# A list scheduler that takes the results of GpSimd's masks as ready later: four graph layers on one core

## The chip, the cores and the metric

The kernel runs on one core of a Trainium2 chip. A core has five engines, each with its own instruction stream: TensorE (PE in the profile, with its weight loads shown apart as PEld), VectorE (DVE), ScalarE (ACT), GpSimd (POOL) and SyncE (SP), which here only issues DMA transfers. The engines run beside each other and wait for each other through semaphores. The metric is the time of one execution on the device in microseconds; the figure for a kernel is the median of its runs.

## The reference

There are 128 small graphs. Each has 128 nodes, 512 features a node in `x`, and a 128 by 128 matrix of edges `adj` of zeros and ones. Four attention layers follow each other, and each ends in a residual sum and a layer norm:

```python
x = _layernorm(x + _L0_gnn_ref(x, adj, ...), axis=-1)   # one head; scores from x itself; mask adj + eye
x = _layernorm(x + _L1_gnn_ref(adj, x, ...), axis=-1)   # 4 heads of 256, elu, then one head of 512; softmax over axis 1
x = _layernorm(x + _L2_gnn_ref(x, adj, ...), axis=-1)   # 8 heads of 64
x = _layernorm(x + _L3_gnn_ref(x, adj, ...), axis=-1)   # one head, elu
```

A layer's attention is, with small differences from layer to layer:

```python
e = leaky_relu(s_src[..., :, None] + s_dst[..., None, :], 0.2)
attn = softmax(where(mask, e, -big))
out = einsum(attn, h)        # h is x or x @ W
```

The mask of the first layer is `adj` with the diagonal added. The second layer normalises over the other axis and so needs the transposed mask, diagonal included. The third and fourth layers take `adj` as it is. All is done in float32.

## The kernel before, in words

One graph is one tile of 128 partitions (its nodes). `graph(g)` (L562) writes down the operations of graph g as a list of objects `Op`: an engine, a cost in microseconds, the buffers read and written, and a function that emits the instructions. There are 188 operations a graph, taken by number in the text where a line is not enough. A program of two stages then lays down one order for all engines.

`Pipeline.plan` (L79) places the operations of one model graph in a period of 28 us (`PERIOD`), so that every engine's operations fit in it without overlap; a graph starts every period, and some 18 graphs are in flight together. It uses the costs and the latencies of the table `LATENCY`. Its results are planned times, one for each operation.

`Pipeline.order` (L145) then walks through all operations of all graphs. It keeps a clock for each engine, and at each step issues the operation that can start first by its own estimate of costs. An operation is ready when the operations it depends on have ended plus a delay from the table `FLOW`: one for readers on the same engine, one for readers on another. It looks at most 30 us ahead of the oldest planned operation not yet issued (`AHEAD`). It also chooses the place of each buffer: a place is free once all users of the buffer before it have ended plus the same delay. Eight places are the banks of PSUM, the others lie in SBUF or, for transposition, in DRAM. The order so found is emitted as it stands: on the chip every engine runs its own instructions in that order, and waits where something is not ready. The estimates have no other effect on the program than the order and the places of buffers.

The parts that matter here:

- `first(g)` (L830) is the first layer. It loads x and adj by SyncE (L834, L835). GpSimd adds the diagonal (L838) and makes two masks with `mask` (L737, instruction L738): m0 from the sum and m2 from adj. TensorE transposes m2 through a product with the identity (L850), VectorE multiplies the result by one minus the identity into m1 (L851). m0 serves the first layer, m1 the two attentions of the second, m2 the eight heads of the third; the fourth layer loads adj again and makes its own mask m3.
- `attend` (L632) is the attention: ScalarE's leaky relu (L641), VectorE's masking with the running minimum (L649, one instruction and one accumulator read a head), ScalarE's exponential with its sum (L658), VectorE's reciprocal (L666), in the second and fourth layers GpSimd's scaling (L668), then the transposition in `turned` (L597): VectorE by blocks of 32 (L602), out to DRAM and back by SyncE (L607, L612, L617).
- `norm` (L673): VectorE's statistics (L676, L677), GpSimd's inverse root (L680, L681), then the scaling on VectorE (L699) or, with a further operation of GpSimd (L688, L692), on ScalarE (L695).
- `project` (L704) multiplies by the weights of the second layer (L710 on w1s) and of the third (L710 on wha, eight products a graph, evicted by VectorE at L715 and ScalarE at L717).
- `halves` (L749) does the second weight matrix of the second layer for two graphs at a time with sums made on GpSimd (L780) and products (L794); `mixed` (L722, instruction L725), L896 and L938 are the products with the attention. GpSimd also adds biases and residuals (L862, L881, L950, L986).
- A product in float32 is two matmul instructions, L850 is one.

In `mask` the operation has a cost of 0.8 and no extra; only SyncE's transfers have one, which `Op.done` (L70) adds to the latency in the plan. In `order` it enters only, through `done`, into how many places the buffers of a kind get.

Of the kernel before, what the change touches and what calls it, by code (L numbers as in the profile page):

```python
# [29 lines left out]

PERIOD = 28.0
LATENCY = {"PE": (0.0, 0.8), "DVE": (0.15, 1.6), "ACT": (0.1, 1.6), "POOL": (0.1, 1.6), "SP": (6.8, 6.8)}
FLOW = {"PE": (0.0, 0.6), "DVE": (0.15, 0.9), "ACT": (0.1, 0.9), "POOL": (0.1, 0.9), "SP": (3.2, 3.2)}
AHEAD = 30.0
URGENCY = 0.3
BANKS = 8
# [24 lines left out]
class Op:  # L61
# [7 lines left out]

    def done(self, reader=None):  # L70
        own, other = LATENCY[self.engine]
        return self.cost + self.extra + (own if reader is self.engine else other)


class Pipeline:
# [69 lines left out]
    def order(self, events):  # L145
# [33 lines left out]
        free = {tag: [(0.0, s) for s in range(BANKS if tag == "ps" else len(p))] for tag, p in free.items()}  # L179
        ready, released, clock, lane = [0.0] * n, {}, {e: 0.0 for e in FLOW}, 0.0  # L180
        known = {e: [i for i in range(n) if not before[i] and ops[i].engine == e] for e in FLOW}
        issued, low, out = [False] * n, 0, []

        def start(i):
            t = max(clock[ops[i].engine], ready[i])
            for b in makes[i]:

                rank = 0
                for q in coming[b.tag]:
                    if q >= i or rank >= len(free[b.tag]):  # L190
                        break
                    rank += 1
                if rank >= len(free[b.tag]):
                    return None
                t = max(t, free[b.tag][rank][0])
            return t

        while len(out) < n:
            best = None
            for e, waiting in known.items():  # L200
                found = None
                for i in waiting:
                    if events[i][0] > events[low][0] + AHEAD and i != low:
                        break
                    t = start(i)
                    if t is not None and (found is None or t < found[0]):
                        found = (t, i)
                        if t <= clock[e]:
                            break
                if found and (best is None or found < best):  # L210
                    best = found
            t, i = best
            op = ops[i]
            known[op.engine].remove(i)
            issued[i] = True
            out.append((events[i][1], op))
            for b in makes[i]:
                b.slot = free[b.tag].pop(0)[1]
                coming[b.tag].remove(i)
            clock[op.engine] = done = t + op.cost  # L220
            own, other = FLOW[op.engine]
            if op.dma:

                done = lane = max(lane, done) + op.dma
                own = other = FLOW["SP"][0]
            for q in after[i]:
                ready[q] = max(ready[q], done + (own if ops[q].engine == op.engine else other))
                before[q] -= 1
                if not before[q]:
                    insort(known[ops[q].engine], q)  # L230
            for b in op.bufs:
                released[b] = max(released.get(b, 0.0), done + other)
                open_uses[b] -= 1
                if not open_uses[b] and b.slot is not None and b.tag != "const":
                    insort(free[b.tag], (released[b], b.slot))
            while low < n and issued[low]:
                low += 1
# [4 lines left out]
def tile_gat_stack(  # L242
# [319 lines left out]
    def graph(g):  # L562
# [3 lines left out]
        def op(engine, cost, emit, ins=(), outs=(), extra=0.0, uses=(), dma=0.0):  # L566
            ops.append(Op(engine, cost, emit, list(ins), list(outs), extra, uses, dma))
# [55 lines left out]
        class Col:  # L623
# [3 lines left out]
            def __call__(self, h=None):  # L627
                if h is None:
                    return self.buf.ap[:, self.a : self.a + self.n]
                return self.buf.ap[:, self.a + h : self.a + h + 1]  # L630

        def attend(db, h0, nh, src, mask, scaled=False):  # L632


# [102 lines left out]
        def mask(m, a, what):  # L737
            op("POOL", 0.8, lambda: nc.gpsimd.tensor_scalar(  # L738
                out=m.ap, in0=a.ap, scalar1=0.0, scalar2=-BIG, op0=what, op1=ALU.mult
            ), [a], [m])  # L740

        def score(xv, wv, init, sc, s):
            jk = Buf("junk", [P, F])
# [86 lines left out]
        def first(g):  # L830
# [7 lines left out]
            op("POOL", 0.6, lambda: nc.gpsimd.tensor_tensor(out=ae.ap, in0=at.ap, in1=eye_i, op=ALU.add), [at], [ae])  # L838

            mask(m0, ae, ALU.is_equal)  # L840


# [3 lines left out]
            score(x0, w0s, b0t, sc0, 0)  # L846
            db = spread(Col(sc0, 1, 1), 1)
            mask(m2, at, ALU.is_le)
            pm = bank()
            op("PE", 0.11, lambda: nc.tensor.transpose(pm.ap[:, :P], m2.ap, ident), [m2], [pm])  # L850
# [138 lines left out]
        if g == B:  # L989

            whole = graph(None)
            a = [op.wait for op in whole].index(-1)
# [12 lines left out]
        a = len(ops)  # L1005
# [45 lines left out]
```

## Time and profile before

| | us |
|---|---|
| median of 3 runs | 3205.73 (3203.74 to 3207.6) |
| profiled execution, its own time | 3213.19 |
| its span in the profile | 3211.2 |
| TensorE busy | 3050.0 (95%) |
| VectorE busy | 2967.3 (92%) |
| ScalarE busy | 2172.0 (68%) |
| GpSimd busy | 2285.5 (71%) |
| DMA, mean busy share in the steady stretch | 0.80 |
| granted clock of TensorE, mean | 0.98 |

The profile is one execution. A group is written as line, engine, operation, and the names of what it writes and reads. A wait is written as "who, line <- released by whom, line: us in total, times, longest". Up to about 200 us the weights are loaded and prepared, and after about 3050 us the last graphs run out; between lies the steady stretch, in which one graph leaves every 23.8 us on average (2850 us over some 120 graphs). In the profile an operation that waits shows the idle time in front of it in square brackets.

### The profile page before, as it was taken

The numbers are of one execution on the slowest core, as the hardware profiler recorded it, in microseconds if no ns is written. First come the engines' busy times: TensorE is split into PE (matmuls) and PEld (weight loads), VectorE is DVE, ScalarE is ACT, GpSimd is POOL, SyncE is SP. The second block draws the span as 40 slices with busy tenths as digits, with TensorE's granted clock in tenths as the row PEclk, the third lists the DMA queues.
The fourth block names the chain that finished last, engine by engine and source line by source line (L and its number), as shares of the span: only waits on it lengthen the run. The fifth ranks groups of instructions, "written<-read, shape, count | busy, mean of one in ns | idle before, by whom it ended". The sixth has DMA issues, their size and how long they took to land. (4 is left out here: it accounts for less than half of the span.)

```text
span 3211.2 us, 62683 instructions
## 1 busy us (share of the span) xinstructions
PE 3050.0 (95%) x14822; PEld 2483.6 (77%) x14822; DVE 2967.3 (92%) x10185; ACT 2172.0 (68%) x7427; POOL 2285.5 (71%) x3211
## 2 busy tenths in 40 slices
PE   7899999999999999999999999999999999999974
PEld 4688877788878878788788787887888878878852
DVE  6978999999999999999999999999999999999985
ACT  1356667677777777777777767777777777777764
POOL 3566777777777777777777777777777777777654
PEclk8999999999999999999999999999999999999985
DMA  4457787787888887888788888887787777878784
GB/s 117 104 147 189 190 196 192 192 202 193 204 192 197 202 194 198 197 197 200 193 198 201 192 203 199 194 204 193 198 200 195 200 197 195 203 190 205 183 192 110
DMA packets 1657572, 606.13 MB, mean 189 GB/s; under 512 B 1311562, under 2 KB 1508170, under 8 KB 1657204
## 3 DMA queue, kind: packets, MB, share of 16 engines
q1 hardware_dynamic: 1655836, 598.97, 75.9%
q8 instruction: 120, 1.97, 0.3%
q14 instruction: 248, 2.03, 0.2%
q0 software_dynamic: 576, 2.10, 0.2%
q10 hardware_dynamic: 792, 1.06, 0.1%
HBM read 374.43 MB, written 227.48 MB: 187 GB/s over the span
## 5 line engine op out<-in xcount | busy, mean ns | idle before, releaser
L658 ACT ACTIVATE w<-w,nm 128x128 f32<-128x128 f32 x1920 | 754.2, 394 | 389.5 <-DVE nm L649 347.3
L710 PE MATMUL ps<-w1s,w 128*128 128x258 f32 x4096 | 940.3, 383 | 7.1 <-DMA w<-scr 7.1
L710 PEld LDWEIGHTS ps<-w1s,w 128*128 128x128 f32 x4096 | 780.7, 191 | 176.8 <-issue 30.0
L794 PE MATMUL ps<-w2s,w 128*128 128x257 f32 x3584 | 872.5, 382 | 8.3 <-POOL w L780 5.8
L649 DVE CUSTOM_DVE_ANT_0 w<-w,w 128x128 f32<-128x128 f32 x1920 | 853.6, 545 | 14.4 <-ACT w L641 12.1
L794 PEld LDWEIGHTS ps<-w2s,w 128*128 128x128 f32 x3584 | 655.7, 190 | 98.1 <-POOL w L780 8.0
L602 DVE STREAM_TRANSPOSE w<-w 128x512 f32<-128x512 f32 (+1 forms) x1024 | 539.2, 540 | 45.9 <-POOL w L668 43.8
L710 PE MATMUL ps<-wha,w 128*128 128x273 f32 x2048 | 518.4, 397 | 4.7 <-DMA w<-scr 4.2
L695 ACT ACTIVATE w<-w,mr,rd 128x512 f32<-128x512 f32 x384 | 311.5, 812 | 298.8 <-POOL mr L688 207.2
L641 ACT ACTIVATE w<-w,xl 128x128 f32<-128x128 f32 x1536 | 480.4, 389 | 35.0 <-DMA w<-row 32.4
L710 PEld LDWEIGHTS ps<-wha,w 128*128 128x128 f32 x2048 | 389.2, 195 | 134.9 <-issue 35.6
L950 POOL TENSOR_TENSOR w<-z,w 128x512 f32<-128x512 f32 x128 | 151.7, 1185 | 348.1 <-DVE z L942 301.1
L680 POOL TENSOR_SCALAR rd<-mv 128x1 f32<-128x1 f32 x512 | 153.3, 299 | 341.2 <-DVE mv L677 184.5
L681 POOL TENSOR_TENSOR rd<-rd,neghalf 128x1 f32<-128x1 f32 x512 | 345.7, 675 | 42.7
L658 ACT ACTIVATION_READ_ACCUMULATOR w<-w,nm 128x1 f32 x1920 | 361.4, 188 | 0.0
L676 DVE BATCH_NORM_STATS2 st<-w 128x6 f32<-128x512 f32 x512 | 340.7, 675 | 10.3 <-POOL w L986 6.3
L717 ACT COPY xl<-ps 128x258 f32<-128x258 f32 (+1 forms) x640 | 226.4, 363 | 153.5 <-PE ps L710 152.7
L881 POOL TENSOR_TENSOR xl<-xl,b1t 128x512 f32<-128x512 f32 x256 | 325.1, 1290 | 0.3
L725 PE MATMUL ps<-w,w 128*128 128x512 f32 x512 | 271.7, 613 | 37.4 <-DMA w<-scr 26.5
L938 PEld LDWEIGHTS ps<-xl,w 128*128 128x128 f32 x2048 | 263.1, 195 | 37.4 <-DVE nm L649 12.8
L649 DVE DVE_READ_ACCUMULATOR2_ANT nm<- 128x1 f32 x1920 | 288.2, 150 | 0.0
L938 PE MATMUL ps<-xl,w 128*128 128x66 f32 x2048 | 256.0, 274 | 18.0 <-DMA w<-scr 11.9
(183 smaller groups left out, 4452.1 us busy)
## 6 DMA issues: line engine op xcount, KB each, us to landing
scr<-w SPq DMA_DIRECT2D x640, 256.0 KB
w<-scr SPq DMA_DIRECT2D x640, 256.0 KB
w<-row SPq DMA_DIRECT2D x128, 512.0 KB
w<-in_x_dram SPq DMA_DIRECT2D x128, 256.0 KB
w<-row SPq DMA_DIRECT2D x128, 256.0 KB
out_dram<-w SPq DMA_DIRECT2D x128, 256.0 KB
w<-row SPq DMA_DIRECT2D x384, 64.0 KB
scr<-w SPq DMA_DIRECT2D x384, 64.0 KB
```

Of the source, the lines that this page charges most:

```text
L602: op("DVE", 0.12 + 0.133 * n, lambda: nc.vector.transpose(zb.ap.rearrange("p b h c -> p h b c"), src.ap.rearrange("p (h b c) -> p h b c", ...
L641: nc.scalar.activation(z.ap[:, h, :], db.ap[:, h0 + h, :], AF.Prelu, bias=src(h0 + h), alpha=SLOPE)
L649: nc.vector.tensor_tensor_reduce(out=zz.ap[:, h, :].rearrange("p (b a) -> p a b", b=4), in0=z.ap[:, h, :].rearrange("p (a b) -> p a b", b= ...
L658: nc.scalar.activation(zz.ap[:, h, :], zz.ap[:, h, :], AF.Exp, bias=nm.ap[:, h : h + 1], scale=-1.0, accum_out=rs.ap[:, h : h + 1],)
L676: op("DVE", 0.6, lambda: nc.vector.bn_stats(st.ap, y.ap), [y], [st])
L681: nc.gpsimd.tensor_tensor(out=rd.ap, in0=rd.ap, in1=neghalf, op=ALU.pow)
L695: op("ACT", 0.6, lambda: nc.scalar.activation(y.ap, y.ap, AF.Identity, bias=mr.ap, scale=rd.ap), [y, rd, mr], [y])
L710: op("PE", w * 4 / 2400 + 0.006, lambda k=k: nc.tensor.matmul(px.ap[:, :w], lhsT=lhs.ap[:, k, :], rhs=wa(k, c), start=(k == 0), stop=(k == ...
L725: op("PE", width * 4 / 2400, lambda: nc.tensor.matmul(pa.ap[:, :width] if len(xv.shape) == 2 else pa.ap.rearrange("p (s c) -> p s c", s=2) ...
L794: return lambda: nc.tensor.matmul(q[b].ap[:, :C2], lhsT=x()[:, k, :], rhs=w2s[:, slot, k, :], start=(fresh and k == 0), stop=(k == 3), ski ...
L881: op("POOL", 1.3, lambda nh=nh: nc.gpsimd.tensor_add(xl.ap[:, nh, : 2 * FH], xl.ap[:, nh, : 2 * FH], b1t[:, nh * 2 * FH : (nh + 1) * 2 * F ...
L938: op("PE", 0.225, lambda u=u, h=h: nc.tensor.matmul(pa.ap[:, u * CH : (u + 1) * CH], lhsT=pt.ap[:, u, :], rhs=xl3.ap[:, h * CH : (h + 1) * ...
```

## The change

The change is in the scheduler's estimates, not in what is computed. GpSimd's delay to readers on other engines in `FLOW` goes from 0.9 to 1.2 us. The masks get an extra of 2.0 us, and `order` adds the extra of a GpSimd operation to the delay for readers on other engines, and so also to the time at which the places of the buffers that the mask uses come free. `Op.done` leaves out the extra of all but SyncE's operations, so that the plan is what it was. Two lines are added in `order`, so that what stands behind them (L222 on) has a number higher by two in the changed kernel: the mask is L740 there, the transposition L852.

```diff
-FLOW = {"PE": (0.0, 0.6), "DVE": (0.15, 0.9), "ACT": (0.1, 0.9), "POOL": (0.1, 0.9), "SP": (3.2, 3.2)}
+FLOW = {"PE": (0.0, 0.6), "DVE": (0.15, 0.9), "ACT": (0.1, 0.9), "POOL": (0.1, 1.2), "SP": (3.2, 3.2)}
...
     def done(self, reader=None):
         own, other = LATENCY[self.engine]
-        return self.cost + self.extra + (own if reader is self.engine else other)
+        return self.cost + (self.extra if self.engine == "SP" else 0.0) + (own if reader is self.engine else other)
...
             clock[op.engine] = done = t + op.cost
             own, other = FLOW[op.engine]
+            if op.engine == "POOL":
+                other += op.extra
...
         def mask(m, a, what):
             op("POOL", 0.8, lambda: nc.gpsimd.tensor_scalar(
                 out=m.ap, in0=a.ap, scalar1=0.0, scalar2=-BIG, op0=what, op1=ALU.mult
-            ), [a], [m])
+            ), [a], [m], 2.0)
```

## The prediction

> **What bounds the kernel now.** I read the busy times first, then the waits of TensorE and VectorE over the steady stretch, then the timeline of one graph. From the head of the page:
>
> ```profile
> PE 3050.0 (95%) x14822; PEld 2483.6 (77%) x14822; DVE 2967.3 (92%) x10185; ACT 2172.0 (68%) x7427; POOL 2285.5 (71%) x3211
> ```
>
> From the table by stages, 200 to 3050 us (length, then busy time of PE, PEld, DVE, ACT, POOL; clock; DMA share):
>
> ```profile
> 200.00:3050.00 2850.00, 2788.19 (x13818) 2295.53 (x13817) 2694.33 (x9289) 2022.73 (x6944) 2112.57 (x2957) 1.00 0.80 196
> ```
>
> TensorE is busy 97.8% of the stretch at full clock, VectorE 94.5%. TensorE is idle 61.8 us, VectorE 155.7. The waits of TensorE in that stretch, all of them:
>
> ```profile
> PE ps L850 <- POOL w L738: 58.4, 101, 2.2
> PE ps L794 <- POOL w L780: 2.4, 3, 1.3
> PE ps L710 <- ACT w L641: 0.3, 1, 0.3
> PE ps L710 <- DMA w<-scr: 0.3, 1, 0.3
> ```
>
> So 58.4 of 61.8 us is one wait, 0.58 us at 101 transpositions of a mask (L850) for GpSimd's mask (L738). That wait is the ceiling of the gain. The waits of VectorE in the same stretch, longest first:
>
> ```profile
> DVE w L602 <- POOL w L668: 40.5, 105, 1.8
> DVE w L699 <- POOL rd L681: 28.3, 57, 0.8
> DVE w L851 <- PE ps L850: 17.0, 38, 0.8
> ...
> DVE xl L715 <- PE ps L710: 7.2, 35, 1.8
> ```
>
> A wait on a busy engine may still be a symptom, so I followed one graph in the timeline (start, length, engine, line):
>
> ```profile
> 1498.87 0.18 DVE L677 BATCH_NORM_AGGREGATE mv<-st 128x2 f32<-128x6 f32 x1
> ...
> 1499.21 0.22 POOL L680 TENSOR_SCALAR rd<-mv 128x1 f32<-128x1 f32 x1 [1.38 <-DVE mv L677]
> ...
> 1506.89 0.66 POOL L738 TENSOR_SCALAR w<-adj 128x128 f32<-128x128 int32 x1
> ...
> 1507.61 0.33 PE L850 MATMUL ps<-ident,w 128*128 128x128 f32 x1 [0.58 <-POOL w L738]
> ...
> 1507.63 1.40 POOL L668 TENSOR_TENSOR w<-w,ri 128x512 f32<-128x512 f32 x2
> ...
> 1507.97 0.29 DVE L851 TENSOR_TENSOR w<-ps,noneye 128x128 f32<-128x128 f32 x1
> ...
> 1508.71 0.90 DVE L602 STREAM_TRANSPOSE w<-w 128x512 f32<-128x512 f32 x2 [0.35 <-POOL w L668]
> ```
>
> VectorE's mean and variance (L677) releases GpSimd at 1499.21. GpSimd then works without a gap through ten operations to the first L668, 1508.71 less 1499.21: 9.50 us. There VectorE, which waited 0.35, starts again (L602) and works without a gap to the next L677 of the same kind, which ends at 1523.27; GpSimd starts at 1523.43. 9.50 + 14.56 + 0.16 = 24.22 us, one graph. This is a closed loop of VectorE and GpSimd without TensorE. TensorE's mask hangs on the same run of GpSimd: L738 ends at 1507.55, L850 starts 0.06 later, and the matmuls behind it end in time for VectorE's L715. The two ways round are nearly equal, and both are tight. Emptying TensorE's wait need therefore not shorten the graph by its length.
>
> **What the Trainium skill says.** "TensorE: Matmul & The Clock Gate", Part 3, The mechanism: matmuls start and end strictly in program order. The trace agrees: the L710 matmuls behind L850 have their data and start only after it, at 1507.77. "Perfetto Trace Analysis", Identifying the Most-Contended Engine: busy matmul time is no good measure of nearness to the limit. Here it is used only to bound idle time, and PEld is at 81% of the stretch. "SBUF — State Buffer", SBUF: two separate sides: VectorE operations with two SBUF inputs and GpSimd share a pair of ports under an exclusive lock. The trace agrees on its scale: L649, median 0.379 us, takes 1.43 beside a GpSimd L780 that began 0.13 earlier.
>
> ```profile
> L649 DVE CUSTOM_DVE_ANT_0 w<-w,w x1920: 334/379/1499, 35.3 to 3189.3; 128x128 f32<-128x128 f32 x192
> ```
>
> The group's mean is 0.545, so 1920 × (0.545 − 0.379) = 319 us of VectorE's busy time is this collision.
>
> **The change, part by part.** No instruction is added or removed, and the planned times stay, because the plan does not see the extra of a mask. Only the order is laid down anew, with a result of GpSimd readable 0.3 us later by other engines, one of a mask 2.3 us later. I compared the built orders over graphs 10 to 117.
>
> TensorE. Before, L850 stands behind one or two of the eight third-layer matmuls (L710 on wha) in 101 of 108 graphs; after, behind four to eight in 73 and in most of the rest further back. One L710 instruction runs 2.93/12 = 0.24 us and each counted matmul is two, so some five more are 5 × 0.48 = 2.4 us, against a wait of 0.58 (longest 2.2). The wait is gone: −58.4 us on TensorE. L850 itself costs the same 0.33 in either place. Of its other readers' distances, the tightest I find is L794 behind L780: 1.5 us before, and where the two now stand, still above 1.2.
>
> VectorE. L851 (0.29, of which 0.08 overlaps) reads the transposition and moves with it: in 88 of 108 graphs it now stands behind L602. Before, it lay under GpSimd's run of 9.50 us and cost nothing; now it lies in the other half of the loop. Other operations move too. Summed with the durations of this trace, VectorE's half grows by 0.53 us per graph on average, and GpSimd's half shrinks by 1.20, because in 27 of 100 graphs L668 now stands ahead of L862, two masks and a root (1.28 + 0.67 + 0.66 + 1.63 + 0.27 and gaps, 4.8 us; 0.27 × 4.8 = 1.3). Net −0.67 per graph. In the other 73 the loop is not shorter but 0.14 longer.
>
> The other 0.3 us. Readers of the roots and of L668 are set back too; for L699, 57 waits of 0.50 each could lose 0.3, 17 us of VectorE. It is not on the loop; I take nothing, with 0 to −17 as bounds.
>
> Queues. GpSimd's operations move by half a place on average, SP's transfers by one and at most by eleven, ScalarE's by 0.7. TensorE starts on loaded operands 3.5 us or more after the issue even in the tight tenth, and a load lands 2.25 us after its issue in the chain that ended last, so a slip of two issues (0.4 each) stays hidden. The buffers are the same in number. One thing is new: before, the order repeats itself every two graphs from about the eighteenth; after, it repeats only every sixteen.
>
> The sum. There are 2850/23.8 = 120 graphs in the stretch. If every graph were as short as TensorE's work allows, the gain is 58 us. If only the 27 in 100 with the shorter run gain, it is 0.27 × 58 = 16. Slack made in these can be carried into the others, as buffers allow several microseconds, so I take the middle: 37 us. Start and end I take at nothing (L850's remaining 2.8 us lie in the first 200 us, where weights are awaited). The profiled execution took 3213.19, span 3211.2 and 2.0 around it; 3213.2 − 37 = 3176. The median of the runs lies 7.5 lower, at 3205.73, which gives 3169.
>
> **The rivals.** (A) The forecast, the wait goes and about two thirds of it shows: 3169, own range 3153 to 3185; chance 0.45. (B) TensorE becomes the only bound, as the loop's mean (−0.67 × 120 = −80) allows: 3206 − 59 = 3147; chance 0.13. For it speaks that nothing else stops TensorE now; against it, VectorE, which would then be 2694/2791 = 96.5% busy. (C) The loop of VectorE and GpSimd alone decides, and TensorE waits the 58 us elsewhere, first at L794 for L780: 3206, within 0.2% (6.4 us, about what a measurement tells from no change); chance 0.1. For it speaks that 73 of 100 graphs keep the ten operations ahead of L668. (D) Slower: VectorE's eight L649 meet GpSimd's L780 and L986 more often. One more long L649 per graph costs 1.05 us, 126 us in all; VectorE's idle time is 155.7 us, of which the waits shown hold 93, so beyond about 0.5 us per graph it comes out at the end. At 1.05 that is 126 − 63, some 60 us, less what A gives: 3205.7 + 60 − 37 = 3229; chance 0.28. For it speaks that L851 now pushes this row of L649 back, and that an order without the rhythm of two graphs meets in every other place; against it, that 302 of the 384 L780 and L986 already meet one. A small gain, 3185 to 3199, keeps 0.04.
>
> **How the numbers follow.** Faster: A, B and the small gain, 0.62. Same: C, 0.10. Slower: D, 0.28. The range 3146 to 3230 leaves out the lowest part of B, 0.06, and the upper half of D, 0.14. A alone has 3153 to 3185.
>
> **What would show it.** In the new profile L850's wait for L740 (the mask's new line) should be under 5 us. The wait of L602 for L668 should be gone in a quarter of the graphs and up to 0.3 longer in the rest. TensorE's idle time in the steady stretch should be 15 to 35 us, now at L794 or at banks. L649's mean should stay at 0.53 to 0.56; above 0.6, D is right. If TensorE idles 55 us or more without L850, C is right. Wrong I would be through the longer repetition: an order that never settles may stop TensorE in a few graphs of each sixteen, which no mean shows.

## The result, and the profile after

The changed kernel takes 3228.94 us (median of 4 runs, 3219.49 to 3230.12) where the kernel before takes 3205.37 in the same comparison (3203.74 to 3207.6): 1.0067 of it, with a 95% interval of 1.0047 to 1.0087. It is slower by about 22 us, where the forecast was 37 us faster. The profiled execution took 3228.24 us, its span is 3226.4.

The line of busy times at the head of the page, of the changed kernel:

```profile
PE 3065.2 (95%) x14822; PEld 2495.3 (77%) x14822; DVE 2994.2 (93%) x10185; ACT 2158.1 (67%) x7427; POOL 2266.9 (70%) x3211
```

The table by stages, 200 to 3050 us, of the changed kernel (length, then busy time of PE, PEld, DVE, ACT and POOL with instructions; clock; DMA share; GB/s):

```profile
200.00:3050.00 2850.00, 2790.83 (x13772) 2297.99 (x13772) 2713.75 (x9252) 1997.23 (x6906) 2088.50 (x2945) 1.00 0.80 195
```

In the same stretch fewer instructions are done: 13772 matmuls instead of 13818, 9252 on VectorE instead of 9289. TensorE is idle 59.2 us (61.8 before), VectorE 136.2 (155.7 before). The longest waits of TensorE in that stretch, of the changed kernel (us in total, times, longest):

```profile
PE ps L940 <- DVE w L984: 15.1, 22, 1.5
PE ps L796 <- POOL w L782: 14.1, 32, 1.7
PE ps L712 <- DMA w<-scr: 11.5, 16, 1.8
PE ps L712 <- DVE nm L651: 5.5, 7, 1.5
PE ps L712 <- DVE z L944: 3.7, 9, 1.0
PE ps L940 <- DMA w<-scr: 2.8, 2, 2.0
PE ps L852 <- POOL w L740: 2.5, 6, 0.8
```

The one wait of 58.4 us for the mask is 2.5 us now. TensorE waits as long as before, at products of the second and third layer, for VectorE, GpSimd and loads from DRAM in turn. Over the whole span it is idle 161.2 us in both profiles; the 15.2 us between the two spans are busy time of the same 14822 matmuls (3065.2 us for 3050.0). Why they are busy longer is not shown (the end of a matmul is modelled in the profile). The granted clock isn't the reason: it is 0.976 to 0.977 in the runs of the changed kernel and 0.977 to 0.982 in those of the kernel before, but it is 0.975 to 0.979 in a kernel of the experiments that is as fast as before (GpSimd's delay of 1.2 alone), and 0.977 to 0.979 in the slowest kernel of all (the extra of the masks alone). The waits of VectorE:

```profile
DVE w L604 <- POOL w L670: 39.6, 51, 1.5
DVE w L746 <- DMA w<-in_x_dram: 24.8, 31, 1.8
...
DVE xl L814 <- PE ps L796: 6.8, 9, 1.5
...
DVE w L701 <- POOL rd L683: 3.3, 7, 0.5
...
DVE w L853 <- PE ps L852: 1.3, 2, 0.7
```

The block transposition waits for GpSimd's scaling half as often (51 times, 105 before) and in total as long (40.5 before). The wait for the load of x was 3.8 us and is 24.8. Of the masking with the running minimum, the line's own view says:

```profile
L651 DVE CUSTOM_DVE_ANT_0 w<-w,w x1920: 328/378/1516, 35.5 to 3208.1; 128x128 f32<-128x128 f32 x192
```

Its mean is 0.556 us (0.545 before). Over the whole span VectorE's busy time grew by 27 us. The largest terms are a sum of 128 by 2 elements (L917, 0.171 us before, 0.592 now, 128 times: 54 us more) and the score products (L746, 1.04 on average before, 0.79 now: 63 us less). And this is how one graph runs now, in the timeline (start, length, engine, line):

```profile
1505.26 0.22 POOL L682 TENSOR_SCALAR rd<-mv 128x1 f32<-128x1 f32 x1 [0.90 <-ACT w L660]
...
1512.61 0.66 POOL L740 TENSOR_SCALAR w<-adj 128x128 f32<-128x128 int32 x1
...
1513.58 1.40 POOL L670 TENSOR_TENSOR w<-w,ri 128x512 f32<-128x512 f32 x2
...
1513.66 0.27 PE L852 MATMUL ps<-ident,w 128*128 128x128 f32 x1
...
1515.33 0.70 DVE L604 STREAM_TRANSPOSE w<-w 128x512 f32<-128x512 f32 x1
...
1516.53 0.28 DVE L853 TENSOR_TENSOR w<-ps,noneye 128x128 f32<-128x128 f32 x1
```

TensorE's transposition (L852) starts without a wait. In this graph GpSimd's run ahead of the scaling is about as long as before, 1505.26 to 1513.58; in 27 of 108 graphs of the new order the scaling stands ahead of the bias sum and other operations. VectorE's masking of the transposition (L853) stands behind the block transposition (L604), where before it stood ahead of it.

The loss isn't made in one place. Counted in order of time, with sixteen matmuls of the third layer's weights (L710 on wha, L712 in the changed kernel) a graph, the last of them starts 5 us later than in the trace before over the first ten graphs, 2 us earlier at graphs 15 to 25, 4 later at 45 to 85, 10 at 97 to 121 and 16 at the last seven (medians). The start is caught up again; some 6 us of the later part fall between graphs 116 and 117, near the end. (The two profiled executions lie 15 us apart, 3228.24 and 3213.19; the one of before was 8 us above the median of its runs.)

### The profile page after: what moved, and what is told of

It is laid out like the page before. It is cut to its first block, busy times and chain, and to the rows that moved or that the text cites. A ratio compares the mean times of both kernels' runs of the same rounds, so it can differ in the third digit from the quotient of the medians.

```text
span 3226.4 us, 62328 instructions
## 1 busy us (share of the span) xinstructions
PE 3065.2 (95%) x14822; PEld 2495.3 (77%) x14822; DVE 2994.2 (93%) x10185; ACT 2158.1 (67%) x7427; POOL 2266.9 (70%) x3211
## 4 chain that ended last, share of the span: by engine, by line
DVE 43%; PE 22%; DMA 15%; issue 7%; POOL 6%; ACT 5%; SPq 2%; DVEq 0%; ACTq 0%; POOLq 0%
DVE w L651 12%; PE ps L712 10%; DVE w L604 8%; PE ps L796 6%; DVE st L678 4%; DMA w<-scr 4%; DMA w<-row 3%; DMA w<-in_x_dram 3%; DVE w L735 3%; DMA scr<-w 3%; ACT w L660 2%; PE ps L727 2%; DVE w L905 2%; DVE w L746 2%; PE ps L898 2%
## 5 line engine op out<-in xcount | busy, mean ns | idle before, releaser
L712 PE MATMUL ps<-w1s,w 128*128 128x258 f32 x4096 | 942.0, 384 | 27.4 <-DMA w<-scr 14.9
L712 PEld LDWEIGHTS ps<-w1s,w 128*128 128x128 f32 x4096 | 780.2, 191 | 176.5 <-issue 20.2
L796 PE MATMUL ps<-w2s,w 128*128 128x257 f32 x3584 | 890.3, 385 | 18.2 <-POOL w L782 16.8
L651 DVE CUSTOM_DVE_ANT_0 w<-w,w 128x128 f32<-128x128 f32 x1920 | 878.5, 556 | 18.2 <-ACT w L643 16.6
L604 DVE STREAM_TRANSPOSE w<-w 128x512 f32<-128x512 f32 (+1 forms) x1024 | 541.8, 541 | 50.6 <-POOL w L670 45.2
L712 PE MATMUL ps<-wha,w 128*128 128x273 f32 x2048 | 511.7, 397 | 16.9 <-DMA w<-scr 10.8
L712 PEld LDWEIGHTS ps<-wha,w 128*128 128x128 f32 x2048 | 383.6, 192 | 148.3 <-issue 39.7
L682 POOL TENSOR_SCALAR rd<-mv 128x1 f32<-128x1 f32 x512 | 138.0, 270 | 361.6 <-DVE mv L679 275.1
L683 POOL TENSOR_TENSOR rd<-rd,neghalf 128x1 f32<-128x1 f32 x512 | 321.4, 628 | 42.7
L940 PE MATMUL ps<-xl,w 128*128 128x66 f32 x2048 | 265.5, 275 | 36.9 <-DMA w<-scr 16.6
```

Source lines behind the costliest of these rows:

```text
L604: op("DVE", 0.12 + 0.133 * n, lambda: nc.vector.transpose(zb.ap.rearrange("p b h c -> p h b c"), src.ap.rearrange("p (h b c) -> p h b c", ...
L651: nc.vector.tensor_tensor_reduce(out=zz.ap[:, h, :].rearrange("p (b a) -> p a b", b=4), in0=z.ap[:, h, :].rearrange("p (a b) -> p a b", b= ...
L683: nc.gpsimd.tensor_tensor(out=rd.ap, in0=rd.ap, in1=neghalf, op=ALU.pow)
L712: op("PE", w * 4 / 2400 + 0.006, lambda k=k: nc.tensor.matmul(px.ap[:, :w], lhsT=lhs.ap[:, k, :], rhs=wa(k, c), start=(k == 0), stop=(k == ...
L796: return lambda: nc.tensor.matmul(q[b].ap[:, :C2], lhsT=x()[:, k, :], rhs=w2s[:, slot, k, :], start=(fresh and k == 0), stop=(k == 3), ski ...
L940: op("PE", 0.225, lambda u=u, h=h: nc.tensor.matmul(pa.ap[:, u * CH : (u + 1) * CH], lhsT=pt.ap[:, u, :], rhs=xl3.ap[:, h * CH : (h + 1) * ...
```

## The experiments

All ratios are to the kernel before, on the same chip, with their 95% intervals; differences in us are worked out from the ratios. Line numbers move with an edit, so the text names the operation.

### Which way round decides: the mask or the scaling

The prediction took two ways round as nearly equal: through the mask and its transposition, and through the scaling and the block transposition. Each is taken away in the old order. First the transposition reads a constant tile, so that it waits for no mask (the second layer's mask is then the same for all graphs):

```diff
+    lone = const.tile([P, P], F32, name="lone")
...
-            op("PE", 0.11, lambda: nc.tensor.transpose(pm.ap[:, :P], m2.ap, ident), [m2], [pm])
+            op("PE", 0.11, lambda: nc.tensor.transpose(pm.ap[:, :P], lone, ident), [m2], [pm])
```

> The kernel before with its order untouched; the transposition L850 reads a constant tile of the mask's size in place of GpSimd's mask, so TensorE has nothing to wait for there (the second layer is computed with that constant mask, the rest as before). Loop theory (VectorE and GpSimd set the rate, and TensorE's 58 us at L850 is slack on one of two equal ways): 3190 to 3206 us, with TensorE idle some 40 to 60 us elsewhere. TensorE theory (its wait is lost time): 3147 to 3160 us.

Measured: 3201.03 us, 0.9975 (0.9965 to 0.9985), that is 8 us less. Waits of TensorE and VectorE in the steady stretch of this kernel:

```profile
DVE w L604 <- POOL w L670: 79.5, 107, 1.8
...
PE ps L796 <- POOL w L782: 22.2, 38, 1.2
PE ps L712 <- DMA w<-scr: 14.8, 28, 1.8
```

The 58 us of TensorE are worth 8. The block transposition's wait for the scaling doubles, from 40.5 to 79.5 us, and TensorE stops elsewhere.

Then GpSimd scales one head of four (three are left unscaled), which shortens its run:

```diff
-                    zz.ap, zz.ap, ri.ap.unsqueeze(2).to_broadcast([P, nh, P])
+                    zz.ap[:, :1], zz.ap[:, :1], ri.ap[:, :1].unsqueeze(2).to_broadcast([P, 1, P])
```

> The kernel before with its order untouched; GpSimd's scaling L668 of the second layer works on one of the four heads (three heads stay unscaled), 0.4 us in place of 1.04, so the run of GpSimd ahead of VectorE's L602 is 0.64 us shorter, while the mask for L850 comes no earlier. Loop theory with two equal ways: 3190 to 3206 us, the way through L850 and L715 still stands. If the way through L668 alone decides: 3206 less up to 0.35 x 105 = 37 us. TensorE theory: 3203 to 3208 us, TensorE's wait at L850 unchanged at 58 us.

Measured: 3177.08 us, 0.9905 (0.989 to 0.992), 30 us less. Waits of this kernel in the steady stretch:

```profile
PE ps L850 <- POOL w L738: 14.4, 22, 1.6
...
DVE w L602 <- POOL w L668: 2.5, 3, 1.4
```

The table by stages of this kernel:

```profile
200.00:3050.00 2850.00, 2818.47 (x13967) 2322.09 (x13966) 2681.08 (x9420) 2061.41 (x7036) 2044.90 (x2999) 1.00 0.81 199
```

The wait at the block transposition is gone, 38 us of it, and TensorE's wait for the mask goes from 58.4 to 14.4 by itself, though nothing was done to the mask. So most of that wait followed from the other way round and didn't set the time. But the 38 us are not simply what comes out at the end. VectorE is not less idle in the stretch (168.9 us, 155.7 before), since it waits more elsewhere. Its busy time over the whole span is 51 us shorter, 2916.5 for 2967.3, most of it at the masking with the running minimum (38 us) and the score products (16 us), which do the same work as before. The edit takes work away from GpSimd, so that these operations may be held up beside it less often, which would be the prediction's collisions. How much of the 30 us is the shorter scaling itself and how much the shorter operations of VectorE was not separated. Both edits together:

> Both edits of the two kernels before it in this call: L850 reads a constant and L668 scales one head of four. Loop theory: only now do both ways get shorter, 3147 to 3175 us, clearly below either alone. TensorE theory: no further than with the constant alone (within 5 us of it).

Measured: 3169.0 us, 0.9876 (0.9862 to 0.9889), 40 us less: about the sum of 8 and 30. The two ways are not equal: less work at the scaling is worth nearly four times what the mask's wait is.

### The transposition alone is moved

In the old order, with nothing else touched, TensorE's transposition goes as far back as its reader allows:

```diff
+    def later(self, out):
...
+            if op.turned == 1:
+                waits[reader[op.outs[0]]] = (g, op)
+                continue
+            if op in waits:
+                moved.append(waits.pop(op))
```

> The kernel before with its order kept but for one thing: each transposition L850 is taken to just ahead of its reader L851 in the order, which on TensorE is two matmul operations (0.98 us) further back in 111 of 128 graphs. Nothing else moves. Loop theory: TensorE's wait falls from 58 to under 15 us, and the time only to 3190 to 3206 us, with the idle time of TensorE at other places. TensorE theory: 3150 to 3165 us. If VectorE's wait for L850 at L851 grows by 0.3 us a graph and counts: 3206 to 3240 us.

Measured: 3207.02 us, 0.9995 (0.9986 to 1.0003). TensorE's wait for the mask falls from 58 to 27.5 us, VectorE's wait for the transposition grows from 17 to 38.4, the time stays. The two waits in this kernel (its lines: the transposition 862, the mask 750, the reader 864):

```profile
PE ps L862 <- POOL w L750: 27.5, 61, 1.1
DVE w L864 <- PE ps L862: 38.4, 62, 1.1
```

Then the reader goes back too, directly behind the block transposition in 103 of 108 graphs, and the transposition stands behind four or five of the third layer's matmul instructions instead of one or two. This is near to what the change does to these two operations (there both go somewhat further back), and the rest of the new order is left out:

```diff
+        for role in ("reader", "transpose"):
...
+                if role == "reader":
+                    to = next((j for j in near if out[j][1].role == "turn"), None)
+                else:
+                    to = next((j - 1 for j in near if out[j][1].role == "reader" and out[j][1].ins[0] in op.outs), None)
```

> The kernel before, with one thing moved in its order: VectorE's masking of the transposition (L851) goes directly behind the block transposition (L602) in 103 of 108 graphs, where it stood two places ahead of it, and TensorE's transposition (L850) stands just ahead of it in the common order, behind four or five of the third layer's matmul instructions instead of one or two. All other operations keep their places and their buffers. Theory one (this move is what the change costs: 0.29 us of VectorE that lay under GpSimd's run now lies in the other half of the loop): 120 x 0.2 to 120 x 0.29, 24 to 35 us more, less the 8 us that TensorE's wait was worth: 1.005 to 1.009. Theory two (the move costs nothing, the loss lies in the rest of the order that was laid down anew): 0.996 to 1.001, with TensorE's wait for the mask gone.

Measured: 3215.87 us, 1.0029 (1.0017 to 1.0041), 9 us more. Waits of this kernel in the steady stretch (its lines: the block transposition 623, the scaling 690, the transposition 872, its reader 874):

```profile
DVE w L623 <- POOL w L690: 87.1, 107, 1.8
...
PE ps L872 <- POOL w L760: 35.7, 67, 0.6
...
DVE w L874 <- PE ps L872: 4.9, 6, 1.2
```

Before, the reader stood ahead of the block transposition: its 0.29 us and its waits (17 us in all) were spent while VectorE had to wait for the scaling anyway. Without them, the wait at the block transposition is 46.6 us longer, which is about 103 x 0.29 = 30 plus the 12 us by which the reader waits less (4.9 for 17.0). The reader itself now runs in the half of the loop that VectorE carries. The result lies between the two theories: of the 24 to 35 us less 8 that the first one counts, a third to a half came out at the end, and TensorE's wait for the mask didn't go, 35.7 us are left of it. But the sign is shown: in the old order this move costs 9 us by itself.

### The two parts of the change, and other sizes of them

GpSimd's delay of 1.2 alone, with no extra for the masks:

```diff
-FLOW = {... "POOL": (0.1, 0.9), "SP": (3.2, 3.2)}
+FLOW = {... "POOL": (0.1, 1.2), "SP": (3.2, 3.2)}
```

> The other part alone: GpSimd's delay 1.2 in place of 0.9, no extra for the masks. L850 stands behind one to three L710 matmuls, so some of TensorE's wait is left; the order repeats every four graphs. GpSimd's ten operations stay ahead of L668 in every graph. If only the masks' extra costs time: 3195 to 3210 us. If this part makes the change slower: 3218 to 3240 us.

Measured: 3208.06 us, 0.9996 (0.9988 to 1.0004). The row of the table by stages of this kernel:

```profile
200.00:3050.00 2850.00, 2794.68 (x13879) 2307.49 (x13878) 2647.50 (x9340) 2040.99 (x6969) 2095.44 (x2975) 1.00 0.80 197
```

VectorE is 47 us less busy than before in the stretch and the time is the same. So VectorE's busy time alone doesn't set the time either.

The extra of 2.0 for the masks alone, with the delay left at 0.9:

```diff
-            ), [a], [m])
+            ), [a], [m], 2.0)
```

> One part of the change alone: the masks' extra of 2.0 us, GpSimd's delay left at 0.9. L850 stands behind five to eight L710 matmuls in 82 of 98 steady graphs, the ten operations of GpSimd stay ahead of L668 in most graphs, L851 stands behind L602 in most. The order repeats every sixteen graphs. If the masks' extra is what makes the change slower: 3218 to 3240 us. If it is the other part: 3200 to 3212 us. If TensorE's wait counted: 3150 to 3175 us.

Measured: 3253.02 us, 1.0131 (1.0116 to 1.0145). The waits of VectorE and TensorE that stand first in this kernel:

```profile
DVE w L604 <- POOL w L670: 78.4, 85, 1.3
PE ps L852 <- POOL w L740: 41.3, 36, 1.9
```

The extra costs 1.3% by itself, and with the delay of 1.2 added 0.67%. With the extra at 2.0 and the delay at 1.0:

```diff
-FLOW = {... "POOL": (0.1, 1.2), "SP": (3.2, 3.2)}
+FLOW = {... "POOL": (0.1, 1.0), "SP": (3.2, 3.2)}
```

> Both parts, but GpSimd's delay at 1.0 in place of 1.2: the order then repeats every two graphs, as before, with L850 behind six or seven L710 matmuls and L851 behind L602 in every graph, and ten operations of GpSimd ahead of L668 in every graph. If the lost repetition made the change slower: 3150 to 3190 us, TensorE's wait gone for good. If the loop through L668 with L851 now in VectorE's half decides: 3205 to 3235 us in spite of the repetition.

Measured: 3216.18 us, 1.0026 (1.0016 to 1.0036). In this order the reader stands behind the block transposition as in the experiment before, in 104 of 108 graphs, while GpSimd's operations stay ahead of the scaling, and the loss of 8 us is the same within the intervals.

These three led to a theory: the order laid down by the changed kernel repeats itself only every sixteen graphs, and the one with the extra alone was taken to do so too. (Compared engine by engine, it repeats every six.) The old order and, with exceptions, the one with a delay of 1.0 repeat every two graphs, the one with the delay of 1.2 alone every four. An order that doesn't settle would be the cause. Three further orders test it, made with the same two edits: the changed kernel with the delay at 1.1, one with the delay at 0.9 and the extra at 1.0, and one with both at 1.0.

> The changed kernel with GpSimd's delay at 1.1 instead of 1.2, the masks' extra left at 2.0. The order laid down repeats itself every four graphs (changed kernel: every sixteen), and the transposition of the mask stands behind five to seven products of the third layer. Theory one (the loss comes from an order that does not settle into a short rhythm): 0.997 to 1.003 of the kernel before. Theory two (the loss comes from setting the masks far back, whatever the rhythm): 1.005 to 1.010, with the wait of VectorE's block transposition for GpSimd's scaling at 39 us or more.

Measured: 3230.7 us, 1.0068 (1.0055 to 1.0082).

> GpSimd's delay at 0.9 as before, the masks' extra at 1.0 instead of 2.0. The order repeats itself every four graphs; the transposition stands behind one to four products. Theory one (short rhythm is harmless): 0.997 to 1.003. Theory two (setting back costs by its size): half of what the extra of 2.0 alone cost, 1.005 to 1.008.

Measured: 3225.52 us, 1.0049 (1.0037 to 1.0061).

> GpSimd's delay at 1.0, the masks' extra at 1.0. The transposition stands behind three to five products in most graphs, but the order does not repeat itself within eight graphs. Theory one (no short rhythm costs): 1.005 to 1.013. Theory two (setting back costs by its size): 1.002 to 1.006.

Measured: 3231.61 us, 1.0062 (1.0045 to 1.0079).

The theory falls: of two orders that repeat every four graphs, one is as slow as the changed kernel and the other nearly so, and the slowest of all repeats every six. What the slower ones of the seven new orders have in common is the extra. The one without it takes as long as before, the six with it are 0.26 to 1.31% slower. The orders laid down show one thing that goes with it: in these six VectorE's reader of the transposition stands behind the block transposition in 102 to 106 of 108 graphs, in the one without the extra in 4. That is the move which cost 9 us alone; what the orders lose beyond that differs, and its cause was not found. Within these six the size of the extra says little: 1.0 gives 1.0049 and 1.0062, 2.0 gives 1.0026, 1.0067, 1.0068 and 1.0131.

### GpSimd's run is made shorter by its order

The prediction counted a gain where the scaling stands ahead of other operations of GpSimd. In the old order, the scaling goes ahead of up to five of GpSimd's operations and the mask of the transposition of up to four:

```diff
+        for role, most in (("scale", 5), ("mask", 4)):
...
+                while j > 0 and past < most and not clash(out[j - 1][1], op) and out[j - 1][1].role != "root":
+                    past += out[j - 1][1].engine == "POOL"
+                    j -= 1
```

> The order of before with two moves on GpSimd alone: the scaling L668 of the second layer is taken up past L862, a root and two masks, so that it follows the fourth operation of the run, not the ninth, and the mask that TensorE transposes is taken up to one or two places behind it. Nothing is left out. Loop theory: VectorE's 40 us at L602 and TensorE's 58 us at L850 both go, and the time falls by what the two edits together gave with less work, 40 us: 3150 to 3175 us. If the time is VectorE's own work, collisions with GpSimd's ports included, and these change with the shift: 3175 to 3210 us. If the mask of the first layer, now 1.7 us later, stops VectorE: above 3210 us.

Measured: 3248.98 us, 1.0127 (1.0114 to 1.014), 41 us more. Waits in the steady stretch of this kernel, one of ScalarE and the longest of VectorE (its lines 714 and 707 are 695 and 688 in the kernel before, 1002 and 1001 are 982 and 981), and the same two in the kernel before:

```profile
ACT w L714 <- POOL mr L707: 218.7, 114, 3.4
...
DVE w L1002 <- ACT w L1001: 101.6, 54, 1.9
```

```profile
ACT w L695 <- POOL mr L688: 186.7, 157, 2.5
...
DVE w L982 <- ACT w L981: 0.4, 1, 0.4
```

The operations that the scaling passed include a norm's offset (L688). The timeline of this kernel shows what follows (start, length, engine, line):

```profile
1494.90 0.27 POOL L707 TENSOR_SCALAR mr<-mv,rd 128x1 f32<-128x1 f32 x1
...
1495.20 0.81 ACT L714 ACTIVATE w<-w,mr,rd 128x512 f32<-128x512 f32 x1 [2.67 <-POOL mr L707]
...
1497.09 0.67 ACT L1001 ACTIVATE w<-ps,minus 128x512 f32<-128x512 f32 x1
...
1497.79 0.69 DVE L1002 SCALAR_TENSOR_TENSOR w<-w,ps 128x512 f32<-128x512 f32 x1 [1.92 <-ACT w L1001]
```

The offset is late, ScalarE's normalisation waits 2.67 us for it, ScalarE's exponential stands behind that in its order, and VectorE waits 1.92 us for the exponential. With the norm's three operations kept first, and the bias sum (L862) and the first layer's mask put last instead:

```diff
+        for role, step, most in (("bias", 1, 5), ("first", 1, 3), ("scale", -1, 1)):
```

> The order of before with moves on GpSimd alone, so that of the run of ten operations the root and offset of the last norm (L680, L681, L688), the scaling L668 and the mask that TensorE transposes come first, and the mask of the first layer and the bias L862 last. L668 ends some 2 us earlier in its run, that mask 0.4 us, and the last norm's offset is not late as it was where L668 was moved past it. Loop theory: VectorE's 40 us at L602 go and most of TensorE's 58 us: 3150 to 3180 us. If the sum of VectorE's work and collisions holds the time: 3185 to 3206 us. If the bias or the first mask, now 2 us later, stops something: above 3210 us.

Measured: 3204.79 us, 0.9989 (0.9981 to 0.9997). The table by stages and the longest waits of VectorE of this kernel:

```profile
200.00:3050.00 2850.00, 2801.71 (x13872) 2300.20 (x13871) 2602.42 (x9323) 2014.61 (x6963) 2107.21 (x2974) 1.00 0.80 197
```

```profile
DVE w L1001 <- ACT w L1000: 61.9, 51, 1.2
DVE w L618 <- POOL w L880: 44.4, 47, 1.0
DVE w L618 <- POOL w L684: 42.9, 56, 0.8
```

VectorE is busy 92 us less in the stretch than in the kernel before, and idle 92 us more. The gain is 4 us. The block transposition (L618) waits twice as long as before, although the scaling it reads (the one of 128x512, L684) is ready earlier. The timeline shows for what (L880 is the bias sum, which this edit put last):

```profile
1499.70 1.04 POOL L684 TENSOR_TENSOR w<-w,ri 128x512 f32<-128x512 f32 x1
...
1502.30 1.27 POOL L880 TENSOR_TENSOR w<-w,b2t 128x512 f32<-128x512 f32 x1
...
1503.61 0.71 DVE L618 STREAM_TRANSPOSE w<-w 128x512 f32<-128x512 f32 x1 [0.98 <-POOL w L880]
```

The scaling ends at 1500.74, the bias sum at 1503.57, and the transposition starts at 1503.61. In every second graph the place into which it writes is the one that a bias sum reads, so that it waits for the bias sum to let go of it, 44.4 us in all. The other 42.9 us are nearly all waits of the fourth layer's small transposition for its own scaling, which stayed at the end of the run. So one wait took the place of another: an earlier scaling was no gain in either form, but neither edit made it earlier alone, as each put something else late.

### The sum of 128 by 2

This sum (two SBUF inputs) has the largest growth on VectorE. It was replaced by an addition of one number a partition, half the sum of the two shifts to each column, as only their sum counts later. The aim was to take it out of the way of GpSimd's operations:

```diff
-            op("DVE", 0.07, lambda: nc.vector.tensor_add(sc2.ap, xl2.ap[:, :, F // 2], shift2.ap), [xl2], [sc2], uses=[shift2])
+            op("DVE", 0.07, lambda: nc.vector.tensor_scalar_add(sc2.ap, xl2.ap[:, :, F // 2], shift2.ap[:, 0:1]), [xl2], [sc2], uses=[shift2])
```

In the changed kernel:

> The changed kernel with one operation of VectorE in another form: the sum of two 128x2 tiles in SBUF at L917, 0.59 us on average there and 0.17 before, becomes an addition of a scalar held in SBUF, with half the sum of the two shifts for each column (the same result). If VectorE's own time with its collisions sets the time of the changed kernel, and L917's is one: 54 us of VectorE less, 3180 to 3210 us. If the collision only moves to the next operation of VectorE, or is not on the path: 3220 to 3235 us.

Measured: 3229.32 us, 1.0063 (1.005 to 1.0075). But the edit didn't do what it was made for. The group of this instruction in this kernel (busy us, mean ns, idle before):

```profile
L922 DVE TENSOR_SCALAR sc<-xl,shift 128x2 f32<-128x2 f32 x128 | 81.1, 634 | 0.1
```

It is as long as the sum was, 634 ns for 592, so this run can't say what the growth of 54 us costs. In the kernel before, as a control:

> The kernel before with the same edit of the 128x2 sum, which there takes 0.17 us. Control: either theory expects 3200 to 3212 us, at most 5 us from the kernel before.

Measured: 3210.33 us, 1.0005 (0.9996 to 1.0013), no difference; there the instruction takes 234 ns for 171. And with the delay of 1.0 and the extra of 2.0:

> Both parts of the change with GpSimd's delay at 1.0, as in the run with that delay, and the edit of the 128x2 sum, which takes 0.56 us there. If collisions set the time: 3165 to 3200 us, faster than the kernel before. If ScalarE's lateness at L904 and GpSimd's at L604 decide: 3205 to 3222 us.

Measured: 3202.51 us, 0.9984 (0.9977 to 0.9991), 14 us less than the same order with the sum. The instruction has a mean of 619 ns here, 560 as a sum, so a shorter instruction is not the reason; the order of all engines is the same, and VectorE's busy time and the list of its waits hardly differ (59.8 for 58.3 us at the block transposition). The two were measured on two chips, each against the kernel before there. Why this one gained is open. It does show that an order with this instruction as long need not be slower than the kernel before.

### Loads of x, and the scaling in the new order

In the changed kernel the score products read a constant weight twice, and so don't wait for x:

```diff
-                out=jk.ap, in0=xv.ap, in1=wv, scale=1.0, scalar=init, op0=ALU.mult, op1=ALU.add,
+                out=jk.ap, in0=wv, in1=wv, scale=1.0, scalar=init, op0=ALU.mult, op1=ALU.add,
```

> The changed kernel, in its own order of work, but VectorE's two score products of the first layer read a constant weight twice instead of x, so that VectorE no longer waits there for the load of x (24.8 us in the changed kernel, 3.8 before). The scores of the first layer are left out of the computation by this. If the late loads of x are what costs: 15 to 25 us less than the changed kernel, 0.999 to 1.002 of the kernel before. If they are slack: 1.005 to 1.008, as the changed kernel, and the wait shows up on another line of VectorE.

Measured: 3234.93 us, 1.0079 (1.0066 to 1.0092). So the late loads of x cost nothing by themselves. Other waits take their place, such as the sum with ScalarE's elu, 3.1 us in the changed kernel:

```profile
DVE w L984 <- ACT w L983: 14.3, 19, 1.7
```

Last, the scaling of one head of four in the changed kernel (the edit of the second experiment):

> The changed kernel, in which GpSimd's scaling (L670) scales one head of the four and leaves three out. The same edit made the kernel before 0.95% faster. Theory one (the changed kernel is bound by the same loop through GpSimd's scaling, only longer): it gains as much, 0.996 to 0.999 of the kernel before. Theory two (in the changed order other waits take turns in setting the end: scratch loads at TensorE, loads of x, VectorE's own queue): it gains less than half of that, 1.002 to 1.007.

Measured: 3202.86 us, 0.9986 (0.998 to 0.9992): 26 us less than the changed kernel, where the same edit took 30 us from the kernel before. The wait at the block transposition in this kernel:

```profile
DVE w L604 <- POOL w L670: 12.8, 22, 0.7
```

It is 26.8 us shorter than in the changed kernel (39.6), about what the time lost, but the profiled execution is the fastest of its 22 runs, 7 us below their median, and in it VectorE is idle only 10 us less over the whole span and busy 22 us less. So the changed kernel too is bound by a way round on which GpSimd's scaling lies. That the microseconds of this one wait are those that come out at the end is not shown: without the mask's wait the same wait was 79.5 us in a kernel that was 8 us faster.

## Why the prediction was wrong

The sign was missed. The time lies within the given range of 3146 to 3230, at its upper edge, which stood for another mechanism (rival D), so that it lies there by luck.

**What bounds the kernel.** That the way round through GpSimd's scaling holds the time was found, and the scaling of one head bears it out in both kernels (30 us and 26 us). "The two ways round are nearly equal, and both are tight" failed. It was read from one graph in the timeline, in which the mask stands directly ahead of the scaling on GpSimd. Both are late there, but taking away the one is worth 8 us and shortening the other 30.

**TensorE.** "The wait is gone: −58.4 us on TensorE" was right for the wait (2.5 us are left) and wrong as a ceiling of the gain. It was slack, from which at most 8 us could be had. TensorE's idle time stayed at 59.2 us, where 15 to 35 were forecast; this was the sign named for rival C, that TensorE would wait elsewhere. C's mechanism is the one that the runs bear out for this part, its time of 3206 is not.

**VectorE's and GpSimd's halves.** This is the step that failed most: "Net −0.67 per graph", from VectorE's half +0.53 and GpSimd's half −1.20. The traces let both halves be measured, over 107 graphs of each: from the first operation of GpSimd behind the two bias sums (L881) to the end of the second layer's scaling, and from there to the next such operation (mean us per graph).

| kernel | GpSimd's half | the other half | sum |
|---|---|---|---|
| before | 9.27 | 14.51 | 23.78 |
| changed | 7.90 | 15.92 | 23.82 |
| scaling and mask taken forward | 4.64 | 19.45 | 24.09 |
| bias sum and first mask put last | 6.34 | 17.33 | 23.67 |
| one head of four scaled | 8.59 | 14.84 | 23.43 |

GpSimd's half shrank by 1.37, near to what was forecast; the other half grew by 1.41, not by 0.53, and the net is 0.04 longer (0.12 over graphs 40 to 116). What GpSimd does ahead of the scaling in the old order doesn't vanish when the scaling goes ahead of it: it is done behind, and the other half is longer by about as much. In the 21 graphs of the changed kernel whose scaling follows the fourth operation of the run, the halves are 4.54 and 20.40. Where all graphs were treated so, 41 us were lost, because ScalarE waited for a norm's offset; where the norms stayed first, 4 us were gained and the transposition waited for the bias sum instead. Work taken away from GpSimd does shorten the sum: 0.68 less in its half and 0.33 more in the other. The forecast counted in VectorE's half only VectorE's own operations, not what GpSimd still has to do there and who waits for it. The wait at the block transposition did become rarer, 51 times for 105, more than the quarter foreseen, but in total it stayed, 39.6 us for 40.5.

The part of the other half that comes from the reader's new place was measured alone: 9 us slower in all. The forecast had named this cost correctly ("before, it lay under GpSimd's run of 9.50 us and cost nothing") and then netted it against the gain that didn't come.

**The sum.** "I take the middle: 37 us" had no measurement behind it. With what the runs measured in place of the terms it is 9 us more for the transposition and its reader together, as moved in the old order, and nothing for the earlier scaling. That gives 3215, some 13 us short of the result.

**The other 0.3 us.** Taken as 0. The delay alone left the time as it was, 0.9996. The wait of the norm's scaling for the root fell by more than the bound of 17 us, from 28.3 to 3.3, and nothing of it is to be seen in the time.

**Queues.** "A slip of two issues stays hidden" was wrong for the waits. Loads are waited for longer: x at VectorE 24.8 us for 3.8, the transposed tiles back from DRAM (`scr`) at TensorE 14.8 for 0.3, the rows of scores (`row`) at ScalarE 142.5 for 49.8. For x it is shown that this is slack; for the other two it was not tried.

**Rival D.** Its time, 3229, is the one measured, but not its sign: L649's mean should have been above 0.6 us and is 0.556. VectorE's other operations grew and shrank by 60 to 75 us each way. Whether the net 27 us are part of the loss isn't settled, since the run meant to take the largest of them away left it in place. That 47 and 92 us less of VectorE's busy time gave nothing in one order and 4 us in another speaks against it. The 319 us that the forecast put down to collisions of the masking are an estimate, mean less median; no run shows what they cost.

**The longer repetition.** Named as what could make the forecast wrong. Orders that repeat every four or six graphs were as slow or slower, so it isn't the cause.

What stays open: 13 of the 22 us, if the 9 us of the old order count as many in the new one, which was not tried. The loss goes with the extra of the masks in the scheduler: all six orders with it were slower and the one without it was not, though one of the six lost its disadvantage when a single instruction took another form. The rest isn't the loads of x. The scaling's earlier place in 27 of 108 graphs is no common cause, since the order with the extra alone has it in 1 graph and is the slowest. Which operations of the new order make the 13 us is not shown.

## What to carry to other kernels

A wait on the busiest engine need not come out at the end: here 58 us of it were worth 8. Before counting such a wait, shorten each way round by itself (here the mask and the scaling), and look at what else the edit shortened. When an operation is put earlier in an engine's order, name what it passes and who waits for that: here what one half of the loop lost in length, the other gained. When one is put later, look whether it stood in a wait that was there anyway: moved out of it, it is no longer free. Orders laid down anew by a list scheduler differed by 1.3% here with nothing but two delays changed, so a change of its estimates is to be judged by what it does to the whole way round, not by the wait that it was meant to remove.

## What the runs showed of the hardware that was not expected

A VectorE addition of a number per partition to 128 by 2 elements was held up beside GpSimd's work as much as the sum of two tensors: 634 ns on average for 592, with 179 at the least and 1274 at the most. In the changed kernel 55 of the 128 sums take over 0.5 us, and 50 of these lie beside GpSimd's bias sum; in the other form it is 54 of 58. They end when GpSimd's operation does, 17 and 25 ns after it at the median. The Trainium skill, "SBUF — State Buffer", SBUF: two separate sides, names two kinds of VectorE operations that share an exclusive lock with GpSimd, those with two SBUF inputs and those in a mode that uses both ports, so the second form need not be an escape. The traces agree as far as the durations and ends go; they don't show the mode.

The same order, with this one instruction in two forms of about the same mean length (560 and 619 ns), took 3216.18 and 3202.51 us, 1.0026 and 0.9984 of the kernel before. The two profiles don't explain these 14 us.
